# Two attention layers on one core: the first layer's projection by seven block products per half, for all images but the first

## The chip, the cores and the metric

The kernel runs on one core of a Trainium2 chip. A core has a matrix engine (TensorE, PE in the profile), three engines for elementwise work (VectorE or DVE, ScalarE or ACT, GpSimd or POOL), a queue for transfers on SyncE (SP) and one on ScalarE, an on-chip memory (SBUF) and a memory for matmul results (PSUM[...]). The metric is the device time of one execution in microseconds, as the median of several runs; a profiled execution gives the trace.

## The reference

Eight images x of 512 channels and 32 x 32 = 1024 tokens, fp32, pass through two attention layers:

```python
# layer 0
h = group_norm(xf, gn_w, gn_b)                      # 32 groups
qkv = einsum('oc,bct->bot', qkv_w, h) + qkv_b       # 8 heads of 64 channels
q, k, v = fake_quant(q), fake_quant(k), fake_quant(v)   # 8 bits, one scale over all images
w = softmax(einsum('bct,bcs->bts', q * scale, k * scale))
a = einsum('bts,bcs->bct', w, v)
x = xf + einsum('oc,bct->bot', proj_w, a) + proj_b[None, :, None]
# layer 1: one head of 512 channels
h = group_norm(x); q, k, v = h @ wq.T + bq, h @ wk.T + bk, h @ wv.T + bv
x = x + (softmax(q @ k.T / sqrt(512)) @ v) @ wp.T + bp
```

The line before layer 1, `x = xf + proj_w a + proj_b`, is layer 0's projection, the step that is changed: per image a product of a 512 x 512 matrix with 512 x 1024 activations, plus bias and residual.

## The kernel before

*Stages.* From 0 to about 612 us the kernel normalises all images and computes q, k and v, whose quantisation needs the extremes over all images first; raw q, k and v lie in HBM. Then layer 1's weights are folded together with its norm's scales, while the attention of image 0 in layer 0 runs. From 761.9 us there is a loop with a period of 242.3 us: layer 1 of image b runs, in it the projection of image b+1, and, in small portions between TensorE's other blocks, the layer-0 attention of image b+2. Each portion (`advance`, four units of 128 keys by two heads) has st (scores from bf16 q and k), an exponential on ScalarE (pt), a split of pt into two fp16 parts (`two`: one by a cast on ScalarE or GpSimd, the other by a subtraction on VectorE), av (the weighted sums) and sm (the row sums). The last image's layer 1 has no attention beside it.

*The projection.* `project(b, bank)`, line 1081, takes a half of 512 tokens at a time (hf), four output chunks of 128 channels (oc) and four input chunks (cc): 16 fp32 matmuls of 128 x 128 by 512 columns into one bank per oc. VectorE empties each bank by one operation that adds the bias and the input x (tile `xts`, called h in the trace, 128x512), SyncE's queue stores it to HBM as `x1_d` (line 1102), and a chore takes the statistics for layer 1's norm (`stats`). Its weights, 1 MB, are loaded for each image by `load_wp` (line 1064) through ScalarE's queue. Between the halves it yields once for a portion of attention. It is called from `first()` in `layer1` (line 1533), which `o_run` (line 1325), the last product of layer 1, calls through `between[0]` in its step 4. In step 5 and 6 of `o_run` the norm of image b+1 (`norm1`, `norm_steps`) goes on in two parts: a small matmul for group means (gps_b), VectorE's offsets, a second such matmul, a power on GpSimd (line 255), a multiplication, and then four operations on h (128x512) for the first half of the tokens. After `o_run`, layer 1 of the next image begins with the block called g (or a).

*Blocks of seven products.* `seven` (line 1178) computes a 2 x 2 block product with seven block multiplications (Strassen's scheme in Winograd's form) into two PSUM banks x and y, used in turn. Each block product is four matmuls of 256 columns when the blocks have two chunks. A drain follows each of them: `keep` copies a running sum away on ScalarE, `add` adds it to a kept one on VectorE, `whole` finishes the last block. Layer 1 uses it for all of its products: a_block (g), v_block2, s_block and o_run.

```python
work = (
    (0, x, True, keep, 0), (1, y, True, add, 0), (2, x, False, keep, 1),
    (3, y, True, keep, 2), (4, x, False, add, 2), (6, y, False, add, 1),
    (5, x, False, whole, None),
)
```

*What sets the order.* [...]VectorE's and ScalarE's order is written out while the program is built by `InOrder` (from line 65): `do` puts an operation at once, at a modelled time; `later` keeps it as a chore with a cost, a time from which it is ready and one by which it is due (`within`); `fill` puts in chores that fit before the next timed operation, earliest possible start first and due time next; `settle(name)` puts all chores of that name at once. Costs are 0.21 us plus 0.957 ns an element (`elements`). Every VectorE and ScalarE operation therefore has the line 86 in the profile, and every matmul of the loop line 201 (`mm`).[...] `load_pair` (line 802) fetches raw q, k and v of the next two heads and leaves two chores each for their quantisation: "qk" for q and k, "qv" for v, both due late (45 us).

*The portion's order.* Yields of -1 or with other negative values make the next portion `dense`: av, sm of two units, then st, then av, sm of the other two; otherwise av of four, sm of four, then st.

*Places.* In layer 1 `vs` holds column sums of v, `gq` those of g, `vt` v itself, `pts` the exponentials of the scores, `kept_u` kept sums; `acc1` is a tile of 128 x 512 for layer 1's row sums, and the weights `wps` lie in the buffer with the tag `sums`.

Of the kernel before, what the change touches and what calls it, by code (L numbers as in the profile page):

```python
# [53 lines left out]
def attn_pair_kernel(  # L54
# [12 lines left out]
    class InOrder:  # L67
# [68 lines left out]
                    return  # L136
                self.begin(best[1])

        def settle(self, what):

            while True:
                i = next((i for i, c in enumerate(self.chores) if c[0] == what), None)
                if i is None:
                    return
                self.begin(i)

    dve, act, pe = InOrder(nc.vector), InOrder(nc.scalar), InOrder(nc.tensor)

    def elements(n):

        return 0.21 + n * 0.957e-3
# [4 lines left out]
    def awaits(t):  # L156

        pe.t = max(pe.t, t + 0.1)
# [130 lines left out]
    with ExitStack() as fast:  # L289
# [774 lines left out]
        def load_wp(b, dma):  # L1064
            wps[b] = l2p.tile([P, CC, C], F32, tag="sums", name=f"wp0_{b}")
            dma(wps[b], w_sq[WP0])

        def wm_tiles(b):

            two = [  # L1070
                ptp1.tile([P, 4, CC // 2, C // 2], F32, tag="p1", name=f"wm_{b}_{n}")
                for n in range(2)
            ]
            wms[b] = [t[:, i : i + 2] for t in two for i in (0, 2)]
            return wms[b]
# [5 lines left out]
        def project(b, bank=bank):  # L1081
# [33 lines left out]
            for k in [k for k in ao if k[0] == b]:  # L1115
                del ao[k]

        K0, K1 = slice(0, CC // 2), slice(CC // 2, CC)
        tt = dve.tensor_tensor

        def quarters(b, hf):

# [52 lines left out]
            dve.later("o", 0.25, spread, pe.t + 4.0, 5.0)  # L1175
            return rs

        def seven(nm, pairs, keep, whole, add, bank=bank):

            nonlocal turn
            turn ^= 1
            x, y = (bank(f"{nm}_{i}").rearrange("p (t n) -> p t n", t=2) for i in range(2))

            def product(n, ps, start):
                left, right = pairs[n]
                k = left.shape[1]  # L1190
                for t in range(2):
                    for i in range(k):
                        mm(
                            ps[:, t, :], lhsT=left[:, i, bass.ts(t, P)], rhs=right[:, i, :],
                            start=start and t == 0 and i == 0, stop=(i == k - 1),
                            skip_group_check=True,
                        )
# [4 lines that stand above are left out]
                (5, x, False, whole, None),  # L1202
            )
            for i, (n, ps, start, out, m) in enumerate(work):
                awaits(free[(i + turn) % 2])
                product(n, ps, start)
                free[(i + turn) % 2] = out(ps) if m is None else out(m, ps)
                yield i + 1

        free = [0.0, 0.0]  # L1210
        turn = 0

        def slots(gq):

# [110 lines left out]
        def o_run(b, hf, vt, vs, ps_, pts, acc, rx, between):  # L1325
# [50 lines left out]
            for step in seven(  # L1376
                nm,
                ((a11, b11), (a12, b21), (s2, t2), (s3, t3), (s1, t1), (s4, b22), (a22, t4)),
                lambda n, ps: act.do(0.59, lambda: act.copy(u[n], ps)), whole, add,
            ):  # L1380
                if step == 1:
                    settle("p2")
                    yield 1
                elif step == 3:
                    settle("p3")
                if step == 2 + (hf == NH - 1 and not final):
                    settle("acc")
                    rs = inverse1(b, hf, acc)
                    rs_there = pe.t + 9.5
                if step == 4:  # L1390
                    finish(0)
                    yield from between[0]()
                elif step == 5:
                    settle("p4")
                    finish(2)
                    yield from between[1]()
                elif step == 6:
                    yield from between[2]()
                    finish(1)
                    settle("o")  # L1400
                    settle("o0")
                    if final and hf == NH - 1:
                        check_sums()
                    if (0, 1) not in rx:
                        load_x1(b, hf, 0, 1, rx)
                elif step == 7:
                    yield 1
                chore()
            if hf == 0 or final:
                settle_o()  # L1410
# [23 lines left out]
        def layer1(b, steps):  # L1434
# [36 lines left out]
            for hf in range(NH):  # L1471
# [50 lines left out]
                    act.t, 14.0,  # L1522
                )
                if last and b + 1 < B:
                    load_wp(b + 1, act.dma_start)
                    load_x2(b + 1, act.dma_start)
                if done >= B:
                    load_x1(b, hf, 0, 1, rx, aop)
# [2 lines left out]
                if b + 1 < B and last:  # L1531

                    def first():
                        nonlocal ahead
                        yield -1
                        yield from project(b + 1, score_bank)
                        yield 2
                        ahead = norm1(b + 1, score_bank)
                        next(ahead)

                    def more():
                        next(ahead)
                        yield from ()

                    between = [first, more, more]
# [117 lines left out]
        for w in fold():  # L1663
            folded += w
            while pos < (folded - F_FIRST) * A_IMAGE / F_FOLD:
                advance()
        load_wp(0, nc.sync.dma_start)
        load_x2(0, nc.sync.dma_start)
        while done < 1:
            advance()  # L1670
# [373 lines left out]
```

## Time and profile before

| | |
|---|---|
| median of 3 runs | 2644.93 us (2644.86 to 2645.33) |
| the profiled execution, its time | 2642.96 us |
| its span in the trace | 2641.2 us |
| TensorE busy, mean granted clock | 2585.6 us, 0.997 |
| VectorE busy | 1880.1 us |
| ScalarE busy | 1256.9 us |
| projection of images 1 to 6 starts at | 1003.54, 1245.87, 1488.12, 1730.38, 1972.64, 2214.91 us |
| projection of image 7 (nothing beside it) | 2447.05 us, 27.47 us long |
| all pj matmuls | 512 records, 223.6 us busy |

How to read it: the busy times overlap, as the engines work side by side. The chain of work that ended last is followed back from the last instruction, each piece to what released it. A group of instructions is named by what it writes and reads (`pj<-ao,wp`), with buffer numbers left out. An fp32 matmul leaves two records. In the time line, a bracket gives the idle time of the engine before an instruction and what ended it.

### The profile page before, as it was taken

What the parts mean: (1) busy time and instruction counts of PE and PEld (TensorE: products, weight loads), DVE (VectorE), ACT (ScalarE), POOL (GpSimd) and SP (SyncE); (2) the same over time, 40 slices, a digit from 0 to 9 for tenths busy, and PEclk for the clock granted to TensorE, in tenths of its full rate; (3) what the DMA queues carried; (4) which work ended last, traced back from release to release, by engine and by line L of the source; (5) the groups of instructions that cost most, each with busy time, mean ns of one, the idle gap of its engine ahead of it and who ended that gap; (6) DMA issues with size and microseconds to landing.
All of it is one profiled execution on the core that took longest, in us unless ns stands there. A gap on an engine that the chain in (4) does not pass through costs nothing.

```text
span 2641.2 us, 33393 instructions
## 1 busy us (share of the span) xinstructions
PE 2585.6 (98%) x13150; PEld 1657.2 (63%) x13150; DVE 1880.1 (71%) x2733; ACT 1256.9 (48%) x1582; POOL 195.7 (7%) x157
## 2 busy tenths in 40 slices
PE   8999999998998999999999999999999999999998
PEld 4655555553235775766577567757665775677687
DVE  7766666658777777877777677778777776776544
ACT  0011111115866664666566566646665665664121
POOL 0000000001110001000100010011001000100000
PEclk9999999999999999999999999999999999999999
DMA  5233322234321132223222321322232123212211
GB/s 203 112 128 112 127 99 101 88 119 152 134 67 41 57 104 89 85 66 110 94 61 77 112 89 57 105 88 85 64 111 95 61 77 112 89 38 79 100 37 38
DMA packets 146887, 241.96 MB, mean 92 GB/s; under 512 B 26528, under 2 KB 92064, under 8 KB 145184
## 3 DMA queue, kind: packets, MB, share of 16 engines
q1 hardware_dynamic: 115872, 181.50, 20.5%
q10 hardware_dynamic: 30848, 58.23, 6.5%
q8 instruction: 105, 1.72, 0.3%
q14 instruction: 62, 0.51, 0.1%
HBM read 152.86 MB, written 86.28 MB: 91 GB/s over the span
## 4 chain that ended last, share of the span: by engine, by line
PE 83%; DVE 8%; ACT 3%; issue 2%; DMA 2%; POOL 1%; SPq 0%; ACTq 0%; DVEq 0%; POOLq 0%
PE s L201 15%; PE qkps L201 13%; PE o L201 12%; PE pj L201 8%; PE av L201 7%; PE v2ps L201 7%; PE vps L201 6%; PE g L201 5%; PE st L201 4%; PE sm L201 4%; ACT pt L86 2%; DVE two L86 1%; DVE sums L86 1%; DVE x L86 1%; DMA out_dram<-x 1%
## 5 line engine op out<-in xcount | busy, mean ns | idle before, releaser
L86 DVE TENSOR_TENSOR two<-pt,two 128x1024 f16<-128x1024 f32 x496 | 596.7, 1219 | 143.6 <-POOL two L909 114.1
L86 ACT ACTIVATE pt<-st,esc 128x1024 f32<-128x1024 f32 x496 | 527.0, 1116 | 355.3 <-PE st L201 335.5
L86 ACT CAST two<-pt 128x1024 f16<-128x1024 f32 x358 | 362.3, 1056 | 8.4 <-issue 5.8
L86 ACT ACTIVATE u<-qkps,qkb 128x512 f32<-128x512 f32 x90 | 61.9, 687 | 500.5 <-PE qkps L201 500.5
L909 POOL CAST two<-pt 128x1024 f16<-128x1024 f32 x128 | 171.0, 1336 | 1553.6 <-PE sm L201 1028.1
L201 PE MATMUL av<-two,v 128*64 128x512 f16 x1984 | 246.0, 383 | 0.0
L201 PE MATMUL s<-g,h 128*128 128x256 f32 x1024 | 234.1, 381 | 0.0
L201 PE MATMUL pj<-ao,wp 128*128 128x512 f32 x512 | 223.6, 595 | 0.0
L201 PEld LDWEIGHTS s<-g,h 128*128 128x128 f32 x1024 | 192.8, 190 | 31.9 <-issue 4.3
L201 PE MATMUL st<-q,k 64*128 64x512 bf16 x1024 | 162.0, 382 | 21.5 <-ACT pt L86 11.9
L201 PEld LDWEIGHTS <-v 128*64 128x64 f16 x1984 | 98.1, 109 | 133.5 <-issue 65.6
L201 PE MATMUL s<-g,sums 128*128 128x256 f32 x768 | 178.4, 381 | 0.2 <-DVE p L86 0.2
L201 PE MATMUL o<-p,v 128*128 128x256 f32 x768 | 175.2, 382 | 1.0 <-DVE p L86 1.0
L201 PEld LDWEIGHTS pj<-ao,wp 128*128 128x128 f32 x512 | 96.1, 190 | 121.3 <-issue 112.7
L201 PE MATMUL qkps<-sums,wa 128*128 128x512 f32 x360 | 164.6, 592 | 0.0
L201 PEld LDWEIGHTS o<-p,v 128*128 128x128 f32 x768 | 144.3, 190 | 27.1 <-issue 5.7
L201 PEld LDWEIGHTS s<-g,sums 128*128 128x128 f32 x768 | 144.7, 190 | 24.2 <-issue 4.1
L201 PE MATMUL qkps<-x,wqkv 128*128 128x512 f32 x304 | 141.1, 603 | 0.8 <-DVE x L86 0.8
L201 PE MATMUL sm<-two,ones 128*32 128x512 f16 x1984 | 137.7, 383 | 0.5 <-ACT rs L86 0.5
L201 PE MATMUL g<-h,wa 128*128 128x256 f32 x512 | 121.7, 386 | 2.1 <-DVE h L86 2.1
L201 PEld LDWEIGHTS <-k 64*128 64x128 bf16 x1024 | 33.9, 94 | 141.6 <-issue 139.1
L201 PE MATMUL v2ps<-wm,h 128*128 128x256 f32 x512 | 119.9, 383 | 0.7
(202 smaller groups left out, 3566.9 us busy)
## 6 DMA issues: line engine op xcount, KB each, us to landing
rs<-rs_d SPq DMA_DIRECT2D x80, 256.0 KB
x<-in_x_dram SPq DMA_DIRECT2D x32, 512.0 KB
raw<-q_d SPq DMA_DIRECT2D x32, 512.0 KB
raw<-k_d SPq DMA_DIRECT2D x32, 512.0 KB
v_d<-v SPq DMA_DIRECT2D x32, 512.0 KB
x_d<-h SPq DMA_DIRECT2D x64, 256.0 KB
x<-x_d ACTq DMA_DIRECT2D x64, 256.0 KB
out_dram<-x SPq DMA_DIRECT2D x64, 256.0 KB
```

The lines of the kernel that those rows point to most:

```text
L86: ins = self.latest = op(*args, **kw).ins
L201: ins = nc.tensor.matmul(ps, lhsT=lhsT, rhs=rhs, **kw).ins
L909: copy(two[:, 0], pt)
```

## The change

`project7` takes the place of `project` for images 1 to 7; image 0 keeps `project`. Per half of the tokens it runs `seven` once: the weights' blocks and their sums a11, a12, s3, a22, s1, s2, s4 on the left, blocks of `ao` (two channel chunks by 256 tokens) and their differences on the right.

* VectorE: eight subtractions of 256 columns for the token differences t1, t2, t3 (in the place of b12) and t4; three adds and three puts of 512; two operations of 256 with bias for `whole`. ScalarE: three keeps of two activations each (128x256, with the bias).
* The differences and kept sums lie in `vs[:, 1]`, `gq[:, 2]`, `gq[:, 3]`, half of `vt` and corners of `pts`, which layer 1's product no longer needs at that point; o_run therefore settles its chore "p4" before the projection.
* The weights' sums are made once, in `make_wp(0)` before the loop: four VectorE operations, and seven stores of 0.25 MB on SyncE's queue into `wp_d`. Per image `load_wp7` loads six of the blocks (1.5 MB, ScalarE's queue, where 1 MB was loaded) and `load_wp7_last` the seventh (SyncE's queue, step 3 of o_run, into the tag `acc1`).
* The result is stored in four pieces per half, 0.25 MB each with rows of 1 KB.
* `settle` can leave a number of chores; `seven` takes a list as a right side and its own `free`; the last step of o_run yields -1 where it yielded 1, except in its first half and for the last image, so that the next portion is dense.

```diff
--- before.py
+++ after.py
@@ -136,13 +136,13 @@
                     return
                 self.begin(best[1])
-        def settle(self, what):
+        def settle(self, what, left=0):
             while True:
-                i = next((i for i, c in enumerate(self.chores) if c[0] == what), None)
-                if i is None:
+                at = [i for i, c in enumerate(self.chores) if c[0] == what]
+                if len(at) <= left:
                     return
-                self.begin(i)
+                self.begin(at[0])
     dve, act, pe = InOrder(nc.vector), InOrder(nc.scalar), InOrder(nc.tensor)
@@ -1065,6 +1065,39 @@
             wps[b] = l2p.tile([P, CC, C], F32, tag="sums", name=f"wp0_{b}")
             dma(wps[b], w_sq[WP0])
+        wp_d = dram.tile([P, 7, CC // 2, C // 2], F32, name="wp_d")
+        def make_wp(b):
+            a11, a12, a21, a22 = (
+                wps[b][:, 2 * k : 2 * k + 2, r * 256 : (r + 1) * 256]
+                for r in range(2) for k in range(2)
+            )
+            s1, s2, s3 = (kept_u[:, i] for i in range(3))
+            s4 = wp_last("made")
+            tt(s1, a21, a22, ALU.add)
+            tt(s2, s1, a11, ALU.subtract)
+            tt(s3, a11, a21, ALU.subtract)
+            tt(s4, a12, s2, ALU.subtract)
+            for i, t in enumerate((a11, a12, s3, a22, s1, s2, s4)):
+                nc.sync.dma_start(wp_d[:, i], t)
+        def wp_last(nm):
+            return l1p.tile([P, C], F32, tag="acc1", name=f"wp0_6_{nm}").rearrange(
+                "p (k n) -> p k n", k=CC // 2
+            )
+        def load_wp7(b):
+            six = l2p.tile([P, 6, CC // 2, C // 2], F32, tag="sums", name=f"wp0_{b}")
+            act.dma_start(six, wp_d[:, 0:6])
+            wps[b] = [six[:, i] for i in range(6)]
+        def load_wp7_last(b):
+            wps[b].append(wp_last(b))
+            nc.sync.dma_start(wps[b][6], wp_d[:, 6])
         def wm_tiles(b):
             two = [
@@ -1115,8 +1148,108 @@
             for k in [k for k in ao if k[0] == b]:
                 del ao[k]
+        tt = dve.tensor_tensor
+        def project7(b, ts, u):
+            settle("ao")
+            st, mvs[b] = stat_tiles(CC, f"b{b}")
+            a11, a12, s3, a22, s1, s2, s4 = wps.pop(b)
+            banks = [0.0, 0.0]
+            parts = []
+            for hf in range(NH):
+                b11, b12, b21, b22 = (
+                    [ao[b, 2 * k + i][:, hf, c * 256 : (c + 1) * 256] for i in range(2)]
+                    for k in range(2) for c in range(2)
+                )
+                t1, t2, t4 = ([t[:, i, :] for i in range(2)] for t in ts[hf])
+                parts.append((b11, b12, b21, b22, t1, t2, t4))
+                for n, (dst, x, y) in enumerate((
+                    (t1, b12, b11), (t2, b22, t1), (b12, b22, b12), (t4, b21, t2)
+                )):
+                    for args in zip(dst, x, y):
+                        dve.later(
+                            f"a{hf}", elements(256), lambda args=args: tt(*args, ALU.subtract),
+                            within=1.0 + 1.5 * n + 16.0 * hf,
+                        )
+            for hf in range(NH):
+                if hf:
+                    yield -1
+                    settle("pj")
+                b11, t3, b21, b22, t1, t2, t4 = parts[hf]
+                whole_rows = []
+                def part(row, col, hf=hf):
+                    c0 = hf * 512 + col * 256
+                    return xts[b][:, 2 * row : 2 * row + 2, c0 : c0 + 256]
+                def bias(e):
+                    return vec[:, V_PB0 + e : V_PB0 + e + 1]
+                def keep(n, ps):
+                    for t in range(2):
+                        there = act.do(0.42, lambda: act.activation(
+                            u[n][:, t, :], ps[:, t, :], AF.Identity, bias=bias(2 * min(n, 1) + t)
+                        ))
+                    return there
+                def store(row, col, hf=hf, part=part, rows=whole_rows):
+                    nc.sync.dma_start(
+                        x1_d[b][row][hf][:, :, col * 256 : (col + 1) * 256], part(row, col)
+                    )
+                    rows.append(row)
+                    if rows.count(row) < 2:
+                        return
+                    for oc in (2 * row, 2 * row + 1):
+                        def stats(oc=oc):
+                            xx = xts[b][:, oc, bass.ts(hf, 512)]
+                            dve.bn_stats(st[:, oc, hf, :], xx)
+                            if hf == NH - 1:
+                                aggregate(mvs[b], st, oc)
+                        dve.later("pj", 0.7 + 0.2 * hf, stats, within=4.0)
+                def add(n, ps, part=part, store=store):
+                    row, col = ((0, 0), (1, 0), (1, 1))[n]
+                    there = dve.do(elements(512), lambda: tt(u[n], ps, u[n], ALU.add))
+                    def put():
+                        xx = part(row, col)
+                        tt(xx, xx, u[n], ALU.add)
+                        store(row, col)
+                    dve.later("pj", elements(512), put, within=4.0)
+                    return there
+                def whole(ps, part=part, store=store):
+                    xx = part(0, 1)
+                    def put():
+                        for t in range(2):
+                            dve.scalar_tensor_tensor(
+                                xx[:, t, :], ps[:, t, :], bias(t), xx[:, t, :], ALU.add, ALU.add
+                            )
+                    there = dve.do(2 * elements(256), put)
+                    store(0, 1)
+                    return there
+                for step in seven(
+                    f"pj_{b}_{hf}",
+                    ((a11, b11), (a12, b21), (s2, t2), (s3, t3), (s1, t1), (s4, b22), (a22, t4)),
+                    keep, whole, add, score_bank, banks,
+                ):
+                    if step in (2, 3, 5):
+                        settle(f"a{hf}", {2: 4, 3: 2, 5: 0}[step])
+                    chore()
+            settle("pj")
+            for k in [k for k in ao if k[0] == b]:
+                del ao[k]
         K0, K1 = slice(0, CC // 2), slice(CC // 2, CC)
-        tt = dve.tensor_tensor
         def quarters(b, hf):
@@ -1175,23 +1308,26 @@
             dve.later("o", 0.25, spread, pe.t + 4.0, 5.0)
             return rs
-        def seven(nm, pairs, keep, whole, add, bank=bank):
-            nonlocal turn
-            turn ^= 1
+        free = [0.0, 0.0]
+        def seven(nm, pairs, keep, whole, add, bank=bank, free=free):
+            free.reverse()
             x, y = (bank(f"{nm}_{i}").rearrange("p (t n) -> p t n", t=2) for i in range(2))
             def product(n, ps, start):
                 left, right = pairs[n]
                 k = left.shape[1]
+                if not isinstance(right, list):
+                    right = [right[:, i, :] for i in range(k)]
                 for t in range(2):
                     for i in range(k):
                         mm(
-                            ps[:, t, :], lhsT=left[:, i, bass.ts(t, P)], rhs=right[:, i, :],
+                            ps[:, t, :], lhsT=left[:, i, bass.ts(t, P)], rhs=right[i],
                             start=start and t == 0 and i == 0, stop=(i == k - 1),
                             skip_group_check=True,
                         )
@@ -1202,13 +1338,10 @@
                 (5, x, False, whole, None),
             )
             for i, (n, ps, start, out, m) in enumerate(work):
-                awaits(free[(i + turn) % 2])
+                awaits(free[i % 2])
                 product(n, ps, start)
-                free[(i + turn) % 2] = out(ps) if m is None else out(m, ps)
+                free[i % 2] = out(ps) if m is None else out(m, ps)
                 yield i + 1
-        free = [0.0, 0.0]
-        turn = 0
         def slots(gq):
@@ -1387,8 +1520,11 @@
                     settle("acc")
                     rs = inverse1(b, hf, acc)
                     rs_there = pe.t + 9.5
+                    if hf == NH - 1 and not final:
+                        load_wp7_last(b + 1)
                 if step == 4:
                     finish(0)
+                    settle("p4")
                     yield from between[0]()
                 elif step == 5:
                     settle("p4")
@@ -1404,7 +1540,7 @@
                     if (0, 1) not in rx:
                         load_x1(b, hf, 0, 1, rx)
                 elif step == 7:
-                    yield 1
+                    yield 1 if hf == 0 or final else -1
                 chore()
             if hf == 0 or final:
                 settle_o()
@@ -1522,7 +1658,7 @@
                     act.t, 14.0,
                 )
                 if last and b + 1 < B:
-                    load_wp(b + 1, act.dma_start)
+                    load_wp7(b + 1)
                     load_x2(b + 1, act.dma_start)
                 if done >= B:
                     load_x1(b, hf, 0, 1, rx, aop)
@@ -1533,7 +1669,12 @@
                     def first():
                         nonlocal ahead
                         yield -1
-                        yield from project(b + 1, score_bank)
+                        yield from project7(
+                            b + 1,
+                            ((vs[:, 1, 0:2], vs[:, 1, 2:4], gq[:, 2]),
+                             (gq[:, 3], vt[:, 0:2, 256:512], vt[:, 2:4, 256:512])),
+                            (pts[0][:, 0:2, 0:256], pts[0][:, 2:4, 0:256], pts[1][:, 0:2, 0:256]),
+                        )
                         yield 2
                         ahead = norm1(b + 1, score_bank)
                         next(ahead)
@@ -1665,6 +1806,7 @@
             while pos < (folded - F_FIRST) * A_IMAGE / F_FOLD:
                 advance()
         load_wp(0, nc.sync.dma_start)
+        make_wp(0)
         load_x2(0, nc.sync.dma_start)
         while done < 1:
             advance()
```

## The prediction

> **What bounds the kernel now.** I read the page's busy times and groups first, then the chain of work that ended last, then a table of one whole period, then the time line around one projection.
>
> From the page, busy time by engine and two of the groups, and from the chain:
>
> ```profile
> PE 2585.6 (98%) x13150; PEld 1657.2 (63%) x13150; DVE 1880.1 (71%) x2733; ACT 1256.9 (48%) x1582; POOL 195.7 (7%) x157
> L201 PE MATMUL pj<-ao,wp 128*128 128x512 f32 x512 | 223.6, 595 | 0.0
> L201 PE MATMUL s<-g,sums 128*128 128x256 f32 x768 | 178.4, 381 | 0.2 <-DVE p L86 0.2
> ```
> ```profile
> 1003.54 13.95 PE pj L201 x32
> 1022.30 13.93 PE pj L201 x32
> ...
> 2447.05 27.47 PE pj L201 x64
> 2485.32 12.09 PE g L201 x56
> ```
>
> TensorE is busy 98% of the span, and the pj matmuls wait for nothing (0.0 idle). The chain names the projection's two halves, so time taken out of TensorE there is time off the end, unless something else comes late. An fp32 matmul leaves two records: the 64 pj records of the last image are 32 matmuls of 512 columns in 27.47 us, 858 ns each, 13.735 us a half; the 56 g records are 28 matmuls of 256 columns in 12.09 us, 432 ns each. That g block is a block of seven products of just the shape that the change gives to a half.
>
> The table of one period (span, then busy time of PE, PEld, DVE, ACT, POOL, then granted clock), and of the stretch right after the projection's image begins its layer 1:
>
> ```profile
> 1003.54:1245.87 242.33, 241.24 (x1398) 160.83 (x1397) 183.29 (x233) 151.48 (x190) 22.80 (x17) 1.00 0.27 86
> 1055.00:1066.00 11.00, 11.00 (x54) 9.07 (x52) 10.96 (x14) 7.45 (x11) 2.51 (x1) 1.00 0.37 134
> ```
>
> Over a period TensorE idles 1.1 us of 242.3 and VectorE 59; but from 1055 VectorE has no idle time either. What it has not done by then delays others. The time line of TensorE, VectorE and GpSimd in the projection of image 1 (start, duration, [idle before]):
>
> ```profile
> 1017.40 0.39 PE L201 MATMUL st<-q,k 64*128 64x512 bf16 x2
> 1018.32 0.39 PE L201 MATMUL st<-q,k 64*128 64x512 bf16 x2 [0.52 <-DVE h L86]
> ...
> 1051.31 0.61 PE L201 MATMUL st<-q,k 64*128 64x512 bf16 x4
> 1051.84 1.92 PE L201 MATMUL av<-two,v 128*64 128x512 f16 x16
> ...
> 1055.21 1.13 PE L201 MATMUL g<-h,wa 128*128 128x256 f32 x4
> ```
> ```profile
> 1019.68 0.75 DVE L86 TENSOR_SCALAR v<-raw,bhi 128x1024 f16<-128x1024 f32 x1
> ...
> 1051.03 0.16 DVE L86 TENSOR_TENSOR grstd_b<-grstd_b,vec 128x4 f32<-128x4 f32 x1 [0.90 <-POOL grstd_b L255]
> 1051.23 1.92 DVE L86 TENSOR_SCALAR h<-h,gmean_b,grstd_b 128x512 f32<-128x512 f32 x4
> 1053.06 0.69 DVE L86 TENSOR_TENSOR kept_u<-o,rs 128x512 f32<-128x512 f32 x1
> ```
>
> The v of the next attention pair is quantised at 1019.68, between the halves, and first read at 1051.84: it has 31 us to spare. The norm's h operations must wait for GpSimd's power until 1051.03.
>
> [...](the trace's pairs of 512 start 0.61 apart, 0.08 under their duration). [...]the operations above stand behind the power although ready ones follow.[...]
>
> **The change part by part.**
>
> *TensorE's own work.* Seven images, 14 halves: 28 matmuls of 256 instead of 16 of 512. In the loop a half takes 13.95 and 13.93, some 0.2 over 13.735, as the first matmuls after attention are slower; I give the new half the same 0.2: 12.09 + 0.2 = 12.29. Gain 13.94 - 12.29 = 1.65 a half, 3.3 an image. The other end for the 0.2 is 0, 1.85 a half.
>
> *Inside a half.* Products alternate between two banks, so each drain must end within the next product (1.73 us each). Bias and keep on ScalarE: two activations, 0.87 us as a pair of that size takes on VectorE; add on VectorE 0.69 and put 0.69; whole 0.87 (the row of two x<-kept_u operations of 256 in this time line). The eight subtractions, 8 x 0.35 = 2.8 us, start with the half and are due from product 3 (t3 and t2) to the last (t4). Walking the new order in VectorE's queue, add0 ends 4.2 us into the half and product 3 on its bank needs it at 5.2; add2 ends at 9.4 and is needed at 10.4. The smallest margin I find is 0.3 us: no stall. [...]the transfer of the last 0.25 MB on SP is behind no load that is due.
>
> *VectorE.* Added per half: 2.8 subtractions + 3 x 0.62 adds + 3 x 0.62 puts + 0.87 whole - 4 x 0.67 for the four evictions = 4.7 us, 9.4 an image. Between 1003.5 and 1053 VectorE idles 15.5 us in all, so the sum fits, but the order changes. ScalarE's added 2.5 us per half lies in stretches where it idles over 10 us.
>
> *After the first half.* The new order of VectorE's instructions puts q and the rest of q's and k's quantising behind `whole`. The score matmul after the half takes over the first bank and waits `whole`: end of half + 0.95 (now the second one waits to + 0.92). The third operation, k, ends at about half + 3.1; now it was done before the half's end. The first matmul with the new k waits until + 3.25 where the block now is at + 2.8, and the next one waits for ScalarE's exponentials. Net +0.55 an image (0.2 to 0.9).
>
> *After the second half.* Here is the main loss. With the additions on VectorE, v's two quantising steps are moved out of the gap between the halves: the second is now in the queue behind the four h operations and behind the `kept_u<-o` of o2's end. And TensorE's order has av right after the four st records that follow o2. Counting from the end of the second half (1036.2 now): TensorE reaches av at 1051.84 - 1036.2 = 15.6. On VectorE the power's result is there at 14.85 as now, h to 16.9, kept_u to 17.5, v to 18.2[...]. TensorE waits 18.25 - 15.6 = 2.65 us. Queued behind the waiting weight load of v is everything of TensorE, the g stage included; VectorE and ScalarE can use the pause only for what is ready. Bounds: 1.9 (if VectorE passes the norm and kept_u 0.7 sooner) to 3.4 (if an attention subtraction of 1.2, less half of it hidden, comes ahead). It cannot gain.
>
> *The rest.* Step 7's order (two pairs of av and sm with st between, not four together) moves no work: 0. GpSimd's order does not change. From 1055 VectorE is as late as TensorE, 1.9 to 3.4 against 2.65, so I add nothing. Six images: -3.3 + 0.55 + 2.65 = -0.1 each, -0.6.
>
> *Image 7.* No attention stands beside it: -3.3, + 0.95 as the second half's first product waits for `whole` of the first at once, + 0.9 as the norm's first matmul waits the last statistics. -1.4.
>
> *Making the weights, once.* Four tensor_tensors of 512, 2.8 us on VectorE, and 1.75 MB of stores on SP's queue ahead of loads, near 625 us. TensorE then has the fold of weights to do; I find the first two's 3 us later and the first exponential that is late 1.2 us, with 2.8 us of slack. 0.5, from 0 to 3.
>
> Sum: -0.6 - 1.4 + 0.5 = -1.5. Of the profiled execution's 2642.96 (span 2641.2 and 1.8 around it) that leaves 2641.5; the median of the runs is 2.0 higher: 2643.5. I take 2644. About 0.2%, 5.3 us, is what a measurement here can tell from no change. The uncertainty of the sum is about 1 us an image: 2637 to 2651.
>
> **The rivals.**
>
> *A. Cancelled, as above*, 2644: 0.42.
>
> *B. The wait for v is small.* If VectorE runs ahead of my walk, or what TensorE loses there it gains in st's present waits for ScalarE (11.9 us in all), 2.2 to 3.3 of 3.3 are kept per image: -13 to -20, likeliest 2629. For it: v's raw data land early, and 15.5 us of idle time precede. Against: the queue is in order and h waits for GpSimd. 0.18.
>
> *C. Slower: the pause halves TensorE's clock.* The trace of before has three long pauses of TensorE:
>
> ```profile
> 807.29 3.75 PE L201 MATMUL g<-h,wa 128*128 128x256 f32 x16 [2.10 <-DVE h L86]
> 814.72 2.62 PE L201 MATMUL g<-sums,wa 128*128 128x256 f32 x8 [3.69 <-ACT two L86]
> ...
> 816.00:818.00 2.00, 2.00 (x7) 1.56 (x6) 2.00 (x4) 0.61 (x2) 0.00 (x0) 0.50 0.81 217
> ```
> ```profile
> 625.40 0.61 PE L201 MATMUL st<-q,k 64*128 64x512 bf16 x2 [2.50 <-ACT pt L86]
> 626.94 5.98 PE L201 MATMUL fold<-wn_h 128*128 128x512 f32 x8
> ```
>
> After 2.10 us the clock stayed 1.00; after 3.69 us it was 0.50 for some 3 us; after 2.50 us, with little work before, eight fold records took 5.98 us, where sixteen took 7.13 at full clock, a loss of 2.4. A pause of 2.65 in otherwise full work lies between. It decides from about 2.5 us on: +2 to +3.5 on each of six images, +12 to +21, likeliest 2659. 0.2.
>
> *D. Slower: VectorE carries its lateness into the full stretch from 1055.* 1 to 2 us an image more: 2650 to 2656, likeliest 2652. For it: image 0's own g stage lost 2.10 and 3.69 us to h and two. Against: in the loop the pause gives VectorE the same time. 0.15.
>
> *E. Making the weights stalls the start* by 3 to 8: 2649. 0.05. That the change does not do what it says is excluded: a listing of each engine's instructions in order has them all.
>
> **How the numbers follow.** A is the likeliest: 2644. Faster by over 0.2%: B 0.18 and a tail of A, 0.06: 0.24. Slower: C 0.2, D 0.13, tails of A and E 0.04: 0.37. Same: 0.39. The range reaches from B's middle to C's middle, 2629 to 2659, leaving out half of each; A's own is 2637 to 2651.
>
> **What would show it.** Right: pj halves of about 12.3 us; a wait of av's weights for v of 2 to 3.4 us after o2 in each of six images; periods within 1 us of 242.3. Wrong: no such wait; a clock under 1.00 at g; idle TensorE inside a half; pauses beyond 1055 after the projection.

## The result and the profile after

The changed kernel takes 2665.52 us (median of 4 runs, 2662.49 to 2665.82), the kernel before 2645.13 us (4 runs): ratio 1.0076, with a 95% interval of 1.0064 to 1.0088. It is slower by 20 us, where no difference was forecast. The profiled execution took 2665.82 us, its span is 2663.9.

From the page, and from the chain of waits for the last image:

```profile
PE 2576.6 (97%) x13486; PEld 1722.5 (65%) x13486; DVE 1943.9 (73%) x2905; ACT 1294.7 (49%) x1666; POOL 191.3 (7%) x157
L201 PE MATMUL pj<-ao,wp 128*128 128x256 f32 (+1 forms) x512 | 132.6, 408 | 6.3 <-ACT pt L86 6.3
```
```profile
2469.30 24.19 PE pj L201 x112
...
2505.37 12.33 PE g L201 x56
```

The multiplications do what they promise: the last image's two halves take 24.19 us instead of 27.47. But TensorE is busy 9 us less in a span that is 23 us longer, and pj now waits for something, ScalarE's pt. The table of one period, and of what follows o2 in it (columns as in the tables above: span, PE, PEld, DVE, ACT, POOL, clock, DMA share, GB/s):

```profile
1005.32:1250.98 245.66, 239.88 (x1449) 170.05 (x1445) 192.36 (x257) 156.90 (x202) 22.57 (x17) 0.99 0.28 88
...
1052.00:1055.30 3.30, 0.00 (x0) 0.00 (x0) 3.26 (x8) 0.91 (x1) 0.00 (x0) 1.00 0.75 210
...
1056.00:1059.00 3.00, 3.00 (x18) 0.46 (x16) 3.00 (x4) 1.81 (x2) 1.55 (x1) 0.50 0.53 175
```

A period is 245.66 us, 3.4 more than before, and TensorE idles 5.8 us of it instead of 1.1. For 3.3 us it stands still while VectorE is busy all the time, and after that its clock is 0.50. The time line of TensorE in the same place as before (between the halves, then after o2):

```profile
1018.64 0.39 PE L201 MATMUL st<-q,k 64*128 64x512 bf16 x2 [0.64 <-DVE h L86]
...
1023.94 3.72 PE L201 MATMUL pj<-ao,wp 128*128 128x256 f32 x16 [1.05 <-ACT pt L86]
...
1051.36 0.61 PE L201 MATMUL st<-q,k 64*128 64x512 bf16 x4
1055.34 1.41 PE L201 MATMUL av<-two,v 128*64 128x512 f16 x8 [3.38 <-DVE v L86]
1056.68 1.04 PE L201 MATMUL sm<-two,ones 128*32 128x512 f16 x8
1057.66 1.04 PE L201 MATMUL st<-q,k 64*128 64x512 bf16 x4
1058.62 1.38 PE L201 MATMUL av<-two,v 128*64 128x512 f16 x8
...
1060.48 1.78 PE L201 MATMUL g<-h,wa 128*128 128x256 f32 x7
```

The two waits are of 1.05 and 3.38 us, and sm of eight records takes 1.04 us where it took 0.62: the half clock. VectorE in front of the longer wait, and ScalarE somewhat earlier:

```profile
1048.18 0.17 DVE L86 TENSOR_TENSOR rcs<-apart 128x16 f32<-128x16 f32 x1 [2.12 <-DMA apart<-rs]
...
1048.55 0.66 DVE L86 TENSOR_SCALAR raw<-raw,rcp 128x1024 f32<-128x1024 f32 x1
...
1049.73 0.15 DVE L86 TENSOR_SCALAR grstd_b<-gps_b 128x4 f32<-128x4 f32 x1
...
1051.92 0.16 DVE L86 TENSOR_TENSOR grstd_b<-grstd_b,vec 128x4 f32<-128x4 f32 x1 [0.90 <-POOL grstd_b L255]
1052.12 1.91 DVE L86 TENSOR_SCALAR h<-h,gmean_b,grstd_b 128x512 f32<-128x512 f32 x4
1053.94 0.68 DVE L86 TENSOR_TENSOR kept_u<-o,rs 128x512 f32<-128x512 f32 x1
1054.55 0.74 DVE L86 TENSOR_SCALAR v<-raw,bhi 128x1024 f16<-128x1024 f32 x1
```
```profile
1041.63 2.25 ACT L86 ACTIVATE pt<-st,esc 128x1024 f32<-128x1024 f32 x2 [0.80 <-DVE two L86]
...
1044.25 0.60 ACT L86 COPY rs<-sm 128x512 f32<-128x512 f32 x1
```

The same two instructions, rcs and the copy of rs, before the change:

```profile
1046.40 0.18 DVE L86 TENSOR_TENSOR rcs<-apart 128x16 f32<-128x16 f32 x1 [1.19 <-DMA apart<-rs]
```
```profile
1042.67 0.61 ACT L86 COPY rs<-sm 128x512 f32<-128x512 f32 x1
```

v stands last in the row rcs, raw, grstd, power, h, kept_u, v. The row also begins late: rcs waits for the small transfer apart, which starts when ScalarE has copied rs, and ScalarE copies it 1.5 us later after the half's end than before (7.96 for 6.44), behind exponentials that wait for `two`. And v's own first step, raw, now stands between rcs and the norm.

One period by its stages, measured at the records' ends; the two right columns are kernels of the experiments:

| us | before | forecast | changed | end alone | whole order |
|---|---|---|---|---|---|
| the two halves | 28.00 | -3.3 | 24.70 | 24.71 | 24.71 |
| between the halves | 4.76 | +0.55 | 6.27 | 6.26 | 4.89 |
| second half to o2's end | 15.14 | 0 | 15.14 | 15.14 | 15.14 |
| o2's end to g | 3.84 | +2.65 | 9.10 | 4.39 | 4.39 |
| the rest | 190.53 | 0 | 190.45 | 190.87 | 190.79 |
| period | 242.27 | -0.1 | 245.66 | 241.37 | 239.92 |

From the first image's loop entry to the last image's projection (1005.32 to 2469.14 now, 1003.47 to 2446.88 before) the changed kernel loses 20.4 us; from there to the last operation ahead of the last transfer it wins 2.0 (186.9 for 188.8). What is left of the profiled execution's 22.9 is 0.5 from the fold of the weights to image 1's projection, and two pieces outside the changed code: 1.4 in a longer wait for the first x, near 14 us, and 2.5 in the last transfer out (7.9 us for 5.4).

### The profile page after: what moved, and what is told of

The parts are those of the page before. It is cut to its first block, busy times and chain, and to the rows that moved or that the text cites. A ratio compares the mean times of both kernels' runs of the same rounds, so it can differ in the third digit from the quotient of the medians.

```text
span 2663.9 us, 34416 instructions
## 1 busy us (share of the span) xinstructions
PE 2576.6 (97%) x13486; PEld 1722.5 (65%) x13486; DVE 1943.9 (73%) x2905; ACT 1294.7 (49%) x1666; POOL 191.3 (7%) x157
## 3 DMA queue, kind: packets, MB, share of 16 engines
HBM read 158.36 MB, written 88.11 MB: 93 GB/s over the span
## 5 line engine op out<-in xcount | busy, mean ns | idle before, releaser
L201 PE MATMUL av<-two,v 128*64 128x512 f16 x1984 | 251.4, 388 | 20.9 <-DVE v L86 20.5
L201 PE MATMUL pj<-ao,wp 128*128 128x256 f32 (+1 forms) x512 | 132.6, 408 | 6.3 <-ACT pt L86 6.3
```

The costliest lines, as they stand in the source:

```text
L201: ins = nc.tensor.matmul(ps, lhsT=lhsT, rhs=rhs, **kw).ins
```

## The experiments

The first theory was W: the wait for v and the half clock that follows are the loss, VectorE has the room. The rival D: VectorE as a whole is too late, so that a wait only changes its name. Times below are set against the kernel before on the same chip (2644.6 to 2645.7 us, 15 to 24 runs each).

### v earlier, after the fourth product

```diff
+                    if hf and step == 4:
+                        settle("qv")
```

> The quantising of the next pair's v is settled in the projection's second half (after its fourth product), so that TensorE finds v ready after o2; all else as in the changed kernel. Theory W (the wait for v, 3.4 us, and the half clock it brings on, 1.8 us, are the loss of each of six images): no wait of av for v, clock 1.00 at g, period 245.7 - 5.2 = 240.5 us, time 2665.8 - 31 = 2635. Rival D (VectorE is late as a whole): the wait only turns up again at g or st under another name, period still over 243.5, time 2653 or more. Rival B2 (v early costs a stall inside the half, 0.3 us of margin against 1.5 us of added VectorE work): period 241.5 to 242.5, time about 2645.

Measured: 2686.83 us, 1.0155 (1.0138 to 1.0172), slower still by 21. The wait for v is gone, but the planner had now put two of attention's subtractions behind the statistics; lines of the waits (total us, times, longest) and one of VectorE's time line show them:

```profile
PE av L201 <- DVE two L86: 24.6, 6, 4.1
...
PE pj L201 <- DVE v L86: 4.5, 6, 0.8
```
```profile
1042.41 5.42 DVE L86 TENSOR_TENSOR two<-pt,two 128x1024 f16<-128x1024 f32 x4
```

The second line of the waits is rival B2's stall, 0.75 us in each image: a product in the second half waits for a token difference that v has delayed. The period was 249.2. W's number fails, and D's seems to hold; but VectorE idled 2.37 and 1.66 us in that same second half. So the question became one of order.

### The wait filled, wholly and in part

TensorE computes one st unit 12 or 3 times more (pad, set after o2's end and 0 elsewhere), into the same place, ahead of av; the other engines' orders are those of the changed kernel.

```diff
-                for i, r in enumerate(HALF):
...
+                for n in range(1 + pad * (u % 2)):
+                    t = pe.t
+                    for i, r in enumerate(HALF):
...
+                    if n:
+                        pe.t = t
+                if u % 2:
+                    pad = 0
```

> The wait for v stays, but TensorE is kept busy in it: the second st unit ahead of av is computed 12 times more into the same place (work added that changes nothing of the result); the order of all other engines is that of the changed kernel. Theory W with the clock as its second part: av starts at the same time, the clock stays 1.00, av to g takes 3.4 us as before the change instead of 5.1, period 245.7 - 1.8 = 243.9, time about 2655. Rival (the slow av, sm and st after the wait have another cause, such as VectorE's or the transfers' load): they stay slow, period 245.7, time 2665.

> As the one before with 3 repeats, some 0.8 us, so that TensorE idles about 2.6 us, the length that the prediction gave the wait. Theory W[...]: the clock stays 1.00, period 243.9, time 2655. Rival (the prediction's own point of 2.5 us): half clock as with 3.4 us, period 245.7, time 2665.

Measured with 12: 2661.19 us (one run); a pause of 0.8 to 0.9 is left, the clock is 1.00 in all six images, o2's end to g is 8.1 instead of 9.1, the period 245.0 (243.9 was expected). So the half clock is real, and costs 1.0 us an image, not the 1.8 that I took for it. With 3: 2665.79 us (one run); pauses of 2.64 to 2.76 us. The table of the three microseconds after the pause in images 1 to 4 (eighth column, after POOL's, the clock):

```profile
1057.00:1060.00 3.00, 2.58 (x24) 0.93 (x26) 3.00 (x3) 1.80 (x2) 1.47 (x1) 1.00 0.56 175
1301.70:1304.70 3.00, 2.57 (x24) 0.92 (x26) 3.00 (x3) 1.79 (x2) 1.45 (x1) 1.00 0.55 175
1546.90:1549.90 3.00, 3.00 (x18) 0.81 (x20) 3.00 (x3) 1.11 (x1) 0.39 (x1) 0.50 0.58 176
1792.35:1795.35 3.00, 3.00 (x18) 0.78 (x20) 3.00 (x3) 1.12 (x1) 0.41 (x1) 0.51 0.55 175
```

The same pause in the same program leaves the clock alone in two images and halves it in four (images 5 and 6 too), where o2's end to g is 9.0 to 9.1 against 8.1. Neither expectation held for all images; what the traces show of the difference is in the last section.

### Seven products for the last image alone

```diff
-                        yield from project7(
+                        yield from project(b + 1, score_bank) if b + 2 < B else project7(
```

with the weights loaded to match.

> Seven products for image 7 alone, where no attention stands beside it; images 0 to 6 use the plain projection with its weights; the weights' sums are made at the start as in the change. Theory W: image 7 gains 1.8 and the making of the weights costs 0.5, no loss in the loop: 2645.0 - 1.3 = about 2643.7. Rival (making the weights costs the whole 1.8 by which the loop started later in the changed kernel): 2645.

Measured: 2648.60 us (12 runs), 1.0013 (1.0004 to 1.0022). The last image wins its 2.0, and from the fold to the first projection it is 1.2 longer in this execution. But the plain loop's period is 243.16, not 242.27: something that both kernels share costs 0.9. I had not expected that.

### The dense order

In the changed kernel undone, and in the kernel before put in alone:

```diff
-                    yield 1 if hf == 0 or final else -1
+                    yield 1
```

> The changed kernel with the last step of o_run yielding 1 as before, so that after o2 all four units of av come, then sm, then st; nothing else. The image-7-only kernel has the plain loop and yet periods of 243.1 us, 0.8 over those before, and in the kernel with the wait filled av to g took 4.2 us against 3.4 at the same clock. Theory: that 0.8 is the dense order, whose second st waits for an exponential; undone, the period goes from 245.7 to 244.9, time about 2661. Rival: with four units first, TensorE waits for the fourth unit's two as well (it ends 1.1 us after v in the changed kernel's VectorE queue), and nothing is won: 245.7, 2665.

> The kernel before the change, with its last step of o_run yielding -1, the only edit. Theory: the dense order alone costs 0.8 a period by the second st's wait for an exponential, 243.1 instead of 242.3, time 2645.0 + 5 = 2650. Rival: the 0.8 of the image-7-only kernel came from the other common edits (p4 settled before the projection, the banks' order), and this one stays at 242.3, 2645.

Measured alone: 2649.85 us (12 runs), 1.0021 (1.0012 to 1.0029); the table of its period:

```profile
1005.15:1248.31 243.16, 241.85 (x1401) 160.67 (x1397) 183.06 (x233) 151.40 (x190) 20.66 (x17) 1.00 0.27 85
```

0.9 a period, 0.55 of them between o2's end and g (4.39 for 3.84): the theory held. Undone in the changed kernel it won nothing in time, 2665.18 us (one run), periods of 244.2 to 245.6, but not for the rival's reason: after o2 TensorE waits for v alone (3.36 to 3.45 us), and for no later `two`. TensorE's av in images 1 and 3, after pauses of the same length:

```profile
1056.97 1.92 PE L201 MATMUL av<-two,v 128*64 128x512 f16 x16 [3.36 <-DVE v L86]
```
```profile
1546.46 3.60 PE L201 MATMUL av<-two,v 128*64 128x512 f16 x16 [3.36 <-DVE v L86]
```

In image 1 the clock stays at 1.00, and o2's end to g is 7.26; the dense order at full clock has 8.09 there (image 1 of the kernel with 3 repeats). So the 0.8 of the theory is won. In the other five images the clock is halved and it is 8.74 to 8.98: the half clock costs 1.4 to 1.7 in this order, where it cost 1.0 in the dense one, and takes back what the order wins.

### v in a gap, and then two as well

```diff
+                    if hf and step == 1:
+                        settle("qv")
```

> The changed kernel with v quantised right after the second half's first product, where the trace of the changed kernel has VectorE idle for 1.57 us, and not after its fourth as in the first experiment, where it pushed two subtractions of attention behind the statistics. In the new order those two stay ahead of the statistics. Theory O (a matter of order, not of load: VectorE has the room, and each misplaced operation becomes a wait of TensorE): no wait for v, clock 1.00 at g, a wait of up to 1 us for the fourth two, which still stands behind h: period 241.5 to 242.5, time about 2645. Rival D (VectorE as a whole is too late): some other wait of 3 us takes its place, period 245 or more, time 2663 or more.

Measured: 2663.11 us, 1.0064 (1.0047 to 1.0080), periods of 244.1 to 245.8. The wait for v is gone and another of the same length has come, as D says. In image 3, TensorE, ScalarE and VectorE:

```profile
1546.65 0.39 PE L201 MATMUL st<-q,k 64*128 64x512 bf16 x2 [3.09 <-ACT pt L86]
```
```profile
1545.48 3.38 ACT L86 ACTIVATE pt<-st,esc 128x1024 f32<-128x1024 f32 x3 [2.84 <-DVE two L86]
```
```profile
1541.50 1.91 DVE L86 TENSOR_SCALAR h<-h,gmean_b,grstd_b 128x512 f32<-128x512 f32 x4
1543.33 0.68 DVE L86 TENSOR_TENSOR kept_u<-o,rs 128x512 f32<-128x512 f32 x1
1543.93 3.73 DVE L86 TENSOR_TENSOR two<-pt,two 128x1024 f16<-128x1024 f32 x3
```

The second st needs the exponential, the exponential the place of a pt that `two` has still to read, and `two` stands behind h, just as v did. In front of h VectorE idles while GpSimd takes the power. So two of them (their chores have the name "sum") were put there, all else as just above (this kernel ran after the whole order below, to take it apart):

```diff
+        at = dve.t + 1.4
+        if nm[0] == "b" and nm != "b0":
+            dve.settle("sum", max(0, len([c for c in dve.chores if c[0] == "sum"]) - 2))
         dve.do(
-            0.15, lambda: dve.tensor_mul(rstd, rstd, vec[:, wcol + c0 : wcol + c0 + n]), dve.t + 1.4
+            0.15, lambda: dve.tensor_mul(rstd, rstd, vec[:, wcol + c0 : wcol + c0 + n]),
+            max(at, dve.t),
         )
```

> The half of the whole order that stands after the projection, alone: v right after the second half's first product and two subtractions of attention in the time of GpSimd's power; q and k stay behind the first half as in the changed kernel. Theory (the losses add up: 4.7 us from o2's end to g, 1.3 us between the halves): o2's end to g falls from 9.1 to 4.4, between the halves it stays 6.27, period 245.66 - 4.7 = 241.0, a little over the 240.0 of the whole order; time 2665 - 28 = about 2637. Rival (with q and k late as well, VectorE has no room before the norm and part of the wait comes back): period over 242, time over 2643.

Measured: 2638.03 us (14 runs), 0.9975 (0.9967 to 0.9983); o2's end to g 4.39. The table of its first period has the clock at 1.00:

```profile
1002.61:1243.97 241.36, 238.69 (x1448) 169.80 (x1444) 191.83 (x257) 156.97 (x202) 21.07 (x17) 1.00 0.28 89
```

### The whole order

The same, with q and k put into the first half, and two of attention's subtractions kept ahead of the second half's statistics:

```diff
+                    if not hf and step in (1, 4):
+                        settle("qk", {1: 3, 4: 0}[step])
+                    if hf and step == 3:
+                        settle("sum", 2)
```

> The changed kernel with four operations ahead in VectorE's queue: k (and q) quantised inside the first half, v after the second half's first product, two of attention's subtractions kept ahead of the second half's statistics, and the next two put into the time of GpSimd's power. No work is added or left out. Theory O: no wait for v or two, between the halves 5 us instead of 6.3, av to g 4.2: period 245.7 - 3.4 - 0.9 - 1.3 = 240, time 2665 - 34 = about 2631, faster than before the change by 0.5%. Rival D: the period stays over 243, time over 2650.

> As the mended order, with the last step of o_run yielding 1 as before the change. Theory O with 0.8 for the dense order: av to g 3.4, period 239.2, time about 2626. Rival: av of four units waits for the fourth two, which ends some 0.5 us after the power: period 240 to 240.5, time 2631 to 2634.

Measured: 2650.56 us (20 runs), 1.0019 (1.0013 to 1.0026), period 243.2; not dense 2655.22 us, 1.0038 (1.0024 to 1.0052), period 244.0. Both miss: all the old waits are gone, and two new ones are inside the second half, for token differences that k had displaced:

```profile
1029.86 1.97 PE L201 MATMUL pj<-v,wp 128*128 128x256 f32 x8 [1.61 <-DVE v L86]
...
1036.56 1.97 PE L201 MATMUL pj<-v,wp 128*128 128x256 f32 x8 [1.28 <-DVE v L86]
```

The one that isn't dense has o2's end to g at 3.83, but a wait of 1.1 for k in each image. The token differences were then named too. (In the norm's edit the limit of two, which the mended order lacks, is there again; the mended order's trace has two subtractions there as well.)

```diff
                     if hf and step == 1:
+                        settle("a1", 4)
                         settle("qv")
                     if hf and step == 3:
                         settle("sum", 2)
+                        settle("a1")
```

> As the mended order, whose remaining loss in the trace is two waits of the second half's products for their own token differences (1.6 and 1.3 us in each image), since the mended order had pushed these back: four of them now stand between the first half's statistics and v, the last ones behind the two subtractions of attention, in gaps of 1.7 and 2.4 us that its trace shows. Again nothing is added or left out against the changed kernel. Theory O: both waits gone, period 243.2 - 2.9 = 240.3, time 2650.6 - 17 = about 2633, faster than before the change by 0.4%. Rival (VectorE has no more room, each operation moved ahead delays another): period 242.5 to 243.2, time 2646 to 2651.

Measured: 2630.34 us (5 runs), 0.9945 (0.9931 to 0.9958): faster than before the change by 14 us, and than the changed kernel by 35, with the same operations. Its time line of TensorE, and its table of a period:

```profile
1024.07 3.72 PE L201 MATMUL pj<-ao,wp 128*128 128x256 f32 x16
...
1052.03 1.05 PE L201 MATMUL av<-two,v 128*64 128x512 f16 x8
...
1055.95 3.72 PE L201 MATMUL g<-h,wa 128*128 128x256 f32 x16
```
```profile
1006.83:1246.80 239.97, 238.54 (x1448) 169.80 (x1444) 191.84 (x257) 156.64 (x202) 21.16 (x17) 1.00 0.29 90
```

None of the three has a wait before it. VectorE is busy 191.84 us a period, as in the changed kernel (192.36). That decides against D: there was room, in the wrong places. Nor are the transfers the loss, with 0.5 MB more of weights an image and stores in rows of 1 KB: the whole order reads and writes the same 158.36 and 88.11 MB as the changed kernel.

## Why the prediction was wrong

The measured 2665.5 us lies at the upper end of rival C (2644 + 21), but that is luck: C's half clock is 6 of the 20 us. Step by step, for each of six images:

*TensorE's own work: right.* -3.30 measured for -3.3; the last image -2.0 for -1.4. The start's 0.5 for 0.5 can't be told from chance: in the same stretch the kernel with the dense order alone took 1.0 us more than the kernel before, and up to there the two have the same instructions in the same order.

*Inside a half: right.* No stall. The 0.35 us for a subtraction of 256 columns was my estimate; in the changed kernel's trace one alone takes 0.41 to 0.42 us, and two in a row 0.75 to 0.76, the second 0.34 after the first (in the first half of image 1).

*After the first half: the term was too small,* 1.5 for 0.55. The walk followed the score matmuls to `whole`, k and the exponential, but stopped there. The second half's first product takes its bank from the same pool as the scores and waits 1.05 us for the exponential that empties it; that one waited for `two`, behind q and k on VectorE. ScalarE's exponential, and VectorE's row:

```profile
1022.77 2.25 ACT L86 ACTIVATE pt<-st,esc 128x1024 f32<-128x1024 f32 x2 [1.05 <-DVE two L86]
```
```profile
1018.51 0.74 DVE L86 TENSOR_SCALAR q<-raw,bhi 128x1024 bf16<-128x1024 f32 x1
1019.17 0.74 DVE L86 TENSOR_SCALAR raw<-raw,rcp 128x1024 f32<-128x1024 f32 x1
1019.95 0.76 DVE L86 TENSOR_SCALAR k<-raw,bhi 128x1024 bf16<-128x1024 f32 x1
1020.61 3.19 DVE L86 TENSOR_TENSOR two<-pt,two 128x1024 f16<-128x1024 f32 x2
```

With q and k in the first half the wait is gone, and the stretch between the halves is 4.89.

*After the second half: the step "TensorE waits 2.65 us" failed, in its size and in what it left out.* The mechanism was there, v behind h behind the power. But "the power's result is there at 14.85 as now" was wrong: it came at 15.6 to 15.7. Two things earlier in the same queue moved it: rcs, which waited for a transfer that ScalarE's later copy had delayed, and v's own first step (raw, 0.66 us); with v in a gap, and raw with it, the same point is reached at 15.2 to 15.4. The wait became 3.4. The late power by itself is not the loss: in the whole order the multiplication after it starts at 15.3 to 15.7 too, with nothing behind it that TensorE waits for. Its lower bound of 1.9 was wrong in kind: with v on time TensorE still waits 3.1, for `two`. I took each wait by itself and asked who else stood behind h only for the v that I had found.

*The clock: rival C's mechanism held, its price did not.* Half clock in all six images, for 1.0 us each where C had 2 to 3.5. C had taken 2.4 from a place where the clock stays at 0.50 for 6.83 us (624.74 to 631.57 before the change); here it stays there for 3.41 us (1055.91 to 1059.32 in image 1), and half of that, 1.7, is my estimate of the most that it can cost. That much is nearly reached in the order that isn't dense; in the dense one the second st waits for an exponential in any case, and part of the cost falls into that wait. Nor did 2.5 us hold as the point from which the clock falls: pauses of 2.71 and 2.73 left it at 1.00 (last section).

*The dense order: "moves no work: 0" failed.* 0.9 a period in the kernel before, 0.55 of it visible in the changed one. An order moves waits even when it moves no work.

The sum: -3.3 + 1.5 + 3.4 (v) + 0.3 (a second st behind it) + 0.55 + 1.0 = +3.45 against 3.39 measured. The parts of o2's end to g are separated by experiments (dense alone; pause filled). The 0.3 is the second st's wait for an exponential at full clock: 0.42 us with the pause filled, 0.14 in the dense order alone.

Open: why the dense order's other 0.34 (the rest of its period) doesn't show in the changed kernel. It does in the two kernels that lost the pause (190.87 and 190.79 in the table).

## What to carry to other kernels

Work that is taken off the bounding engine at the price of more small operations on a second one is won only if the second one's order is planned anew; here the same operations were worth +20 us in one order and -14 in another. When an operation is found late behind a wait of its engine, as v was here (at 1054.55, behind the 0.90 us for the power, h and kept_u), list everything that stands behind that wait, not only the one found, and look for the idle time in front of it: mending one alone only shows the next. And follow a late engine one more link, to the transfers and banks that hang on it.

## What the hardware showed

The length of a pause alone does not tell here whether TensorE's clock falls. In the kernel with 3 repeats pauses of 2.71 and 2.73 us (images 1 and 2) left it at 1.00, and 0.50 followed those of 2.74 and 2.64 (images 3 and 4). A pause of 3.36 left it alone in the kernel that isn't dense (image 1), while 0.50 followed all six of 3.37 to 3.48 in the changed kernel.

In the clock of the traces before and after the change, a stretch of half clock lasts 3.41 us, or twice that (6.83 from 624.74 and from 625.84), but for the last one, at the program's end (8.01 and 9.29). In the changed kernel's loop these stretches begin at 1055.91, 1301.67, 1547.43, 1793.19, 2038.95 and 2284.71 us, 245.76 apart, which is 72 times 3.413; the earlier ones, at 625.84, 810.15 and 816.98, are 126, 72 and 70 times 3.413 ahead of the first of the six. Three of them, each with the 3.41 us ahead of it (the number after the comma is TensorE's busy time, the eighth column the clock):

```profile
806.74:810.15 3.41, 1.54 (x13) 0.84 (x14) 2.61 (x5) 1.39 (x2) 1.74 (x2) 1.00 0.02 5
810.15:813.57 3.42, 3.42 (x10) 2.70 (x9) 3.42 (x4) 1.86 (x2) 0.00 (x0) 0.50 0.00 0
...
1052.50:1055.91 3.41, 0.57 (x6) 0.36 (x8) 3.41 (x7) 0.41 (x1) 0.00 (x0) 1.00 0.56 145
1055.91:1059.32 3.41, 3.41 (x22) 0.64 (x20) 3.38 (x4) 2.13 (x3) 1.87 (x1) 0.50 0.46 154
2281.31:2284.71 3.40, 1.00 (x12) 0.39 (x14) 3.40 (x7) 0.00 (x0) 0.00 (x0) 1.00 0.22 47
2284.71:2288.12 3.41, 3.41 (x22) 0.89 (x20) 3.38 (x5) 2.92 (x3) 2.66 (x1) 0.50 0.45 155
```

Two pauses of the kernel with 3 repeats in pieces of the same length, image 1 (a pause of 2.71 us) and image 3 (2.74), 143 times 3.413 apart:

```profile
1055.12:1058.53 3.41, 1.53 (x16) 0.49 (x17) 3.41 (x6) 0.36 (x1) 0.00 (x0) 1.00 0.48 121
1058.53:1061.94 3.41, 2.99 (x27) 1.36 (x24) 3.38 (x4) 3.37 (x4) 3.31 (x1) 1.00 0.31 119
...
1543.23:1546.64 3.41, 0.93 (x10) 0.19 (x4) 3.14 (x7) 1.11 (x1) 0.20 (x1) 1.00 0.52 154
1546.64:1550.05 3.41, 3.16 (x18) 0.82 (x20) 3.41 (x4) 1.11 (x1) 0.54 (x1) 0.50 0.52 156
```

A border of two pieces falls into the first pause, and most of the second lies in one piece. With the traces before and after the change divided so from end to end, half clock follows eleven pieces at full clock between 20 and 2630 us, with 0.57 to 1.54 us of work in them; every other piece at full clock there has 1.76 or more. It followed 1.54 here and not the 1.53 of image 1 above, so no sharp limit is shown; nor did it follow the first pieces of the program, up to 14.8 us, with 0 to 1.17 us of work. That the place of a pause in these pieces decides is my reading of these cases. It fits the changed kernel: its period, 245.66 us, is 0.1 short of the 245.76, and TensorE's work in the piece ahead of half clock grows from 0.57 us in image 1 to 1.00 in image 6, with half clock after all six.
